# A graph layer on one core: 48 instead of 42 edge tiles gathered row by row, and another order of loads and writes on SyncE's queue

## The chip, the cores and the metric

The kernel runs on one core of a Trainium2 chip. The metric is the device time in microseconds of one execution; lower is better. The core's engines are named as the profile names them: PE (TensorE, with PEld its weight loads), DVE (VectorE), ACT (ScalarE), POOL (GpSimd) and SP (SyncE). PEq, ACTq, POOLq and SPq are the instruction queues of the engines; SP does no arithmetic here and only issues transfers.

## The reference

A message-passing layer over 6,250 nodes and 206,250 edges, sorted by receiver (`dst`), 128 channels in 8 heads of 16. Cut to what matters:

```python
w_ij  = silu(edge_feats @ rad_W1 + rad_b1) @ rad_W2 + rad_b2
w_ij += silu(chi_scalar @ sph_W1 + sph_b1) @ sph_W2 + sph_b2
q_i, k_j, v_j = (x @ Wq)[dst], (x @ Wk)[src], (x @ Wv)[src]
alpha = (q_i * w_ij * k_j).sum(per head) / sqrt(16) * edge_weight
out = segment_sum(alpha * v_j, dst) / 16
result = layernorm(x + out)
```

All arithmetic that matters is float32.

## The kernel before

**Tiles.** 128 edges are a tile, four tiles a quad (403 quads), four quads a group (101 groups). The main loop runs over groups `g` and, in each, over four slots, which take the quads in the order 0, 2, 1, 3 (`order`, line 138). Instructions go onto each engine's queue in the order in which the Python text emits them; each queue is worked off in order, so that an instruction that waits holds everything behind it on its queue.

**A quad.** `first_layers` (PE, `ph`) and `silus` (ACT) make the hidden edge features, `q_at_edges` (PE, `pq`) spreads the receivers' queries over the edges with the one-hot matrix `hotT`, `weigh` (PE, `pw`) makes the edge weights, `multiply`, `scores` and `messages` (DVE) make the messages out of `pq`, `pw` and `kv`, and a group later `sum_quads` (PE, `po`) adds them up by receiver. `sum_group`, `part_sums`, `moments`, `roots` and `normalize` finish a group's 128-row block of the result; four blocks are normalized together.

**Senders' rows.** K and V of all nodes lie as 1 KB rows in a DRAM table `kv_tab`, made in the prologue. For each tile POOL issues one indirect transfer (`gather`, line 132) that fetches 128 rows. `gathers` issues a quad's four tiles 14 quads ahead of their use (`AHEAD`), into a ring of 16 quads (`RING`). The first ten quads get K and V from gathered rows of `x` instead, in the prologue.

**Tiles loaded singly.** In `ROW_TILES` quads, spread evenly over the places 20 to 392 of the order (`row_at`, line 139), the fourth tile isn't gathered: `gathers` issues three transfers, and `load_rows` has the 128 rows fetched by 128 transfers of one row each (line 191, tile `wide`). SP issues 80 of them in batches of 32, 32 and 16, each behind a load of the addresses into registers (`at_i`, line 186); ACT issues 48 in two batches of 24, a few in each slot: two between its two SiLUs (`next_rows(2)`) and up to `ROW_SLOT_ACT - 2` at the end of the slot (`rows_at_end`). A tile's single rows are issued over the slots since the tile before it, ending eight slots ahead of its use (`ROW_LEAD`).

**The rest of SP's queue.** In each group SP also issues `load_x` (slot 0: a register load of the group's place from `gb_i`, line 280, then 64 KB of `x`), `load_feats` (slot 2, three groups ahead, 512 KB), `load_rel` (slot 2, two groups ahead, the receivers `relb`, 128 KB, from which DVE makes `hotT` in `one_hots_T`, line 264, in slot 1 of the group before the one that uses it), and `write_rows` (line 708: one finished block of 64 KB in every slot as long as there is one). Blocks are written at places that may overlap, so each write waits until the write before it has landed. `load_x` and `load_feats` also wait for a matrix product of the slot before (`past`).

Of the kernel before, what the change touches and what calls it, by code (L numbers as in the profile page):

```python
# [12 lines left out]
F32 = mybir.dt.float32  # L13
BF16 = mybir.dt.bfloat16
# [7 lines left out]
SP = mybir.EngineType.SP  # L22
# [3 lines left out]
P = 128  # L26
N = 6250
D = 128
# [7 lines left out]
NG = math.ceil(E / (P * GT))  # L36
NT = NG * GT
EG = P * GT
EQ = P * QT
# [6 lines left out]
ROW_BYTES = 2 * D * 4  # L46
XQ = 10
RING = 16
ROW_TILES = 42
ROW_FIRST = 20  # L50
ROW_LAST = 392
ROW_LEAD = 8
ROW_UNIT = 32
ROW_ACT = 48
ROW_UNIT_ACT = 24
ROW_SLOT_ACT = 6
ROW_SEMS = 8
CHECK = 20
XL = 3
NEIGHBORS = 16.0  # L60
EPS = 1e-5
SCALE = 1.0 / (math.sqrt(HD) * NEIGHBORS)


@with_exitstack
def gnn_kernel(ctx, tc, x, src, dst, weight, edges, rad_W1, rad_b1, rad_W2, rad_b2,
# [14 lines left out]
    nc = tc.nc  # L81
# [11 lines left out]
    src_x = const.tile([P, math.ceil(XQ / NQ) * GT], I32, name="src_x")  # L93
    at_i = const.tile([ROW_TILES, P], I32, name="at_i")
    scale = const.tile([P, NT], F32, name="scale")
# [14 lines left out]
    gb_i = const.tile([1, NG], I32, name="gb_i")  # L110
# [8 lines left out]
    gp = ctx.enter_context(tc.tile_pool(name="group", bufs=2))  # L119
# [18 lines left out]
    order = [g * NQ + j for g in range(NG) for j in (0, 2, 1, 3) if g * NQ + j < QUADS]  # L138
    row_at = [ROW_FIRST + (n + 1) * (ROW_LAST - ROW_FIRST) // ROW_TILES for n in range(ROW_TILES)]
    row_quads = {order[i] for i in row_at}  # L140
# [10 lines left out]
    def rows_at_end():  # L151
        n = ROW_SLOT_ACT - 2
        m = min(n, len(act_now))
# [6 lines left out]
    r_of = {}  # L160
    feats_of, relb_of, act_of, kv_of, hot_of, hotT_of, x_of, q_of, msg_of = ({} for _ in range(9))
# [11 lines left out]
    def load_rows(i):  # L173

        k = next((k for k in range(ROW_TILES) if i <= row_at[k] - ROW_LEAD), None)
        start = len(order) if k is None else (row_at[k - 1] if k else ROW_FIRST) - ROW_LEAD + 1
# [45 lines left out]
    def load_feats(g, mark=None):  # L222
        feats_of[g] = gp.tile([P, EG // 2], F32, name="feats", bufs=3)
        o = nc.sync.dma_start(feats_of[g], edges[g])
        if mark is not None:
            tc.add_manual_dep(o.ins, mark.ins.name, WAIT, reason="one signal of TensorE a quad")
# [3 lines left out]

    def load_rel(g):

        relb_of[g] = gp.tile([P, EQ], BF16, name="relb")
        r = rel_lin[g * GT:(g + 1) * GT, :].rearrange("(j t) e -> j (t e)", j=NQ)
        nc.sync.dma_start(relb_of[g], r[:, None, :].to_broadcast([NQ, W, EQ]))

# [40 lines left out]

    def load_x(g, mark=None):

        r_of[g] = nc.values_load(gb_i[:1, g:g + 1], engines=(SP,), min_val=0, max_val=(N - P) * D * 4,  # L280
                                 skip_runtime_bounds_check_because="the table is clamped to it")
        x_of[g] = gp.tile([P, D], F32, name="x", bufs=XL + 4)
        o = nc.sync.dma_start(x_of[g].bitcast(U8), rows_from(x, r_of[g]))
        if mark is not None:
            tc.add_manual_dep(o.ins, mark.ins.name, WAIT, reason="one signal of TensorE a quad")
# [21 lines left out]
    with tc.tile_pool(name="nodes", bufs=1) as nodes, \  # L307
# [76 lines left out]

        rows_f = nodes.tile([P, ROW_TILES], F32, name="rows_f")

# [6 lines left out]
        def turn_rows():  # L393
            pt = nps.tile([P, QT, P], F32, name="pt", bufs=3)
            nc.tensor.transpose(pt[:ROW_TILES, 0, :], rows_f, ident)
            nc.vector.tensor_copy(at_i, pt[:ROW_TILES, 0, :])

# [64 lines left out]
        n = len(chunks)  # L462
# [49 lines left out]
    with tc.tile_pool(name="ps", bufs=1, space=PSUM) as pp:  # L512
# [27 lines left out]
        def first_layers(q):  # L540

            return [hidden_of(q, i) for i in range(2)][-1]
# [162 lines left out]
        def write_rows(n=1):  # L705
            for _ in range(min(n, len(written))):
                g, y = written.pop(0)
                nc.sync.dma_start(rows_from(out, r_of.pop(g)), y.bitcast(U8))
# [24 lines left out]
        written = []  # L733
        load_feats(1)
        load_rel(1)
        load_feats(2)
        for g in range(1, XL):
            load_x(g)
# [7 lines left out]
        for g in range(NG - 1):  # L746
            for slot, j in enumerate((0, 2, 1, 3)):
                q = g * NQ + j
                i = g * NQ + slot
                turned, past, old = None, mark, marks  # L750
                if slot == 0 and g == CHECK + len(checks) + 1:
                    verdict()
                if slot == 0:
                    turned = turn_q(g + 1, pp.tile([P, EQ], F32, name="pq", bufs=2))
                if slot == 1 and 2 <= g:
                    turned = sum_group(g - 2)
                if slot == 2:
                    turned = make_q(g + 1, pp.tile([P, EQ], F32, name="pq", bufs=2))
                if 1 <= g:
                    for t in ((), (0, 1), (2,), (3,))[slot]:  # L760
                        mark = sum_quads(g - 1, t)
                first_layers(order[i + 2])
                mark = q_at_edges(order[i + 1])
                marks = weigh(order[i + 1])
                silus(order[i + 2], mark, marks, lambda: next_rows(2))
                if turned:
                    turned()
                if 1 <= g and slot == 3:
                    part_sums(g - 1)
                if i + AHEAD < len(order):  # L770
                    gathers(order[i + AHEAD], old[-QT:])
                multiply(order[i + 1], mark)
                messages(q, scores(q, marks=marks), marks=marks)
                if slot == 0:
                    if g + XL < NG:
                        load_x(g + XL, past)
                if slot == 2:
                    if g + 3 < NG:
                        load_feats(g + 3, past)
                    if g + 2 < NG:  # L780
                        load_rel(g + 2)
                if slot == 1:
                    one_hots_T(g + 1)
                    if g + 2 < NG:
                        pick(g + 2)
                    if 1 <= g:
                        place(g - 1)
                write_rows()
                if slot == (3 if g < NG - 2 else 2):
                    if 2 <= g:  # L790
                        statistics(g - 2)
                if slot == 3:
                    if g + 1 < NG - 1:
                        one_hots(g + 1)
                    if CHECK <= g < CHECK + len(checks):
                        checks[g - CHECK]()
                if g == NG - 3 and slot in (0, 2):
                    wide_one_hots(order[slot // 2 - 3])
                if g == NG - 2 and slot == 0:
                    wide_one_hots(order[-1])  # L800
                    n = nc.values_load(general, min_val=0, max_val=1)
                    place(g)
                    place(NG - 1)
                if g == NG - 3 and slot in (1, 3):
                    weigh_wide(order[slot // 2 - 3])
                if g == NG - 2 and slot == 1:
                    weigh_wide(order[-1])
                load_rows(i)
# [56 lines left out]
    def general_group(g):  # L865
        with tc.tile_pool(name="lg", bufs=1) as lg, tc.tile_pool(name="lb", bufs=1) as lb, \
# [12 lines left out]
            for j in range(NQ):  # L879
                kv = lb.tile([P, QT, 2 * D], F32, name="kv_l")  # L880
# [41 lines left out]
                for t in range(QT):  # L922


                    d = dstf_g[:, j * QT + t:j * QT + t + 1]
                    pd = pp.tile([P, P], F32, name="pd")
                    nc.tensor.transpose(pd, d.to_broadcast([P, P]), ident)
                    same = lb.tile([P, P], F32, name="same")
                    nc.vector.tensor_scalar(same, pd, d, None, op0=OP.is_equal)
                    earlier = lb.tile([P, P], F32, name="earlier")  # L930
                    nc.vector.tensor_tensor(earlier, same, before, op=OP.mult)
                    to = lb.tile([P, 4], F32, name="to")
                    nc.vector.tensor_reduce(to[:, 0:1], earlier, AX.X, OP.max)
                    nc.vector.tensor_tensor(to[:, 1:2], spare, d, op=OP.subtract)
                    nc.vector.tensor_tensor(to[:, 2:3], to[:, 1:2], to[:, 0:1], op=OP.mult)
                    to_i = lb.tile([P, 1], I32, name="to_i")
                    nc.vector.tensor_tensor(to_i, to[:, 2:3], d, op=OP.add)
                    ps = pp.tile([P, D], F32, name="ps_l")
                    nc.tensor.matmul(ps, same, msg[:, t, :], start=True, stop=True)
                    part = lb.tile([P, D], F32, name="part_l")  # L940
                    nc.scalar.activation(part, ps, AF.Copy)
                    scatter_add(to_i, part)
# [72 lines left out]
```

## Time and profile before

| | |
|---|---|
| median of 3 runs | 1985.53 us (1983.56 to 1986.35) |
| the profiled execution's own time | 1985.41 us |
| its span in the profile, first to last instruction | 1983.3 us |
| busy: PE / POOL / DVE / ACT | 1782.5 / 1488.6 / 1471.1 / 752.2 us |
| gathers of `kv` and of `x` rows on POOL | 1530 and 40 |
| single rows issued by SP and by ACT | 3360 and 2016 |
| register loads of SP for these rows / for `x` | 126 / 101 |
| granted TensorE clock | 0.916 |

Busy time counts instructions of the engine proper; the issuing of transfers by SP and ACT is not in it, and POOL's busy time holds its gathers without what lies between them. A line in the list of waits reads: engine and line that waited, what it waited for, microseconds in total, number of times, longest. A timeline line reads: start, microseconds, engine, line, operation, tiles and number, and in brackets the idle time before it with what ended it.

### The profile page before, as it was taken

The numbers are of one execution on the slowest core, as the hardware profiler recorded it, in microseconds if no ns is written. First come the engines' busy times: TensorE is split into PE (matmuls) and PEld (weight loads), VectorE is DVE, ScalarE is ACT, GpSimd is POOL, SyncE is SP. The second block draws the span as 40 slices with busy tenths as digits, with TensorE's granted clock in tenths as the row PEclk, the third lists the DMA queues.
The fourth block names the chain that finished last, engine by engine and source line by source line (L and its number), as shares of the span: only waits on it lengthen the run. The fifth ranks groups of instructions, "written<-read, shape, count | busy, mean of one in ns | idle before, by whom it ended". The sixth has DMA issues, their size and how long they took to land.

```text
span 1983.3 us, 55295 instructions
## 1 busy us (share of the span) xinstructions
PE 1782.5 (90%) x16014; PEld 1505.7 (76%) x16014; DVE 1471.1 (74%) x3123; ACT 752.2 (38%) x1437; POOL 1488.6 (75%) x1580
## 2 busy tenths in 40 slices
PE   9899999978997988998898888899989988898897
PEld 7788788767876877876787777777767777777786
DVE  6687777768876877776777777767767767777777
ACT  3244344333343343342343333333433433433334
POOL 7777777777777777777777777777777777777775
PEclk9899899978998998998999889989989999898988
DMA  8545545455455555454554555545545455445543
GB/s 316 160 141 156 157 145 156 142 157 156 143 157 154 146 156 154 144 160 139 159 158 140 159 142 155 158 143 154 154 145 158 144 152 159 142 142 158 157 140 90
DMA packets 150194, 304.77 MB, mean 154 GB/s; under 512 B 38732, under 2 KB 83900, under 8 KB 149884
## 3 DMA queue, kind: packets, MB, share of 16 engines
q0 software_dynamic: 74720, 203.26, 36.7%
q1 hardware_dynamic: 69632, 95.45, 14.8%
q10 hardware_dynamic: 5532, 2.47, 0.5%
q8 instruction: 128, 2.10, 0.4%
q14 instruction: 182, 1.49, 0.3%
HBM read 287.58 MB, written 13.46 MB: 152 GB/s over the span
## 4 chain that ended last, share of the span: by engine, by line
PE 56%; DMA 17%; DVE 11%; issue 6%; POOL 3%; ACTq 2%; SPq 2%; ACT 2%; DVEq 0%; POOLq 0%
PE pw L565 28%; DMA kv<-kv_tab,src_i 14%; PE pq L527 10%; PE ph L518 7%; PE po L616 4%; DVE kq L577 4%; DMA relb<-rel_lin 3%; PE pw L560 3%; ACTq L191 2%; POOL msg L132 2%; DVE side L587 2%; DVE kq L585 2%; SPq L191 1%; PE pq L657 1%; POOL kv L132 1%
## 5 line engine op out<-in xcount | busy, mean ns | idle before, releaser
L132 POOL DMA_INDIRECT kv<-kv_tab,src_i x1530 | 1447.9, 946 | 466.6 <-PE pw L565 174.2
L548 ACT ACTIVATE act<-ph,b 128x512 f32<-128x512 f32 x806 | 546.5, 687 | 1091.0 <-PE pq L527 1003.5
L565 PEld LDWEIGHTS pw<-w,act 128*128 128x128 f32 x6448 | 822.8, 207 | 105.6 <-issue 94.7
L565 PE MATMUL pw<-w,act 128*128 128x128 f32 x6448 | 902.7, 298 | 0.0
L527 PE MATMUL pq<-q,hotT 32*128 32x128 f32 x3224 | 502.9, 299 | 50.8 <-DVE hotT L264 40.4
L518 PE MATMUL ph<-feats,w 32*128 32x512 f32 x1612 | 501.2, 680 | 31.5 <-ACT act L548 30.6
L527 PEld LDWEIGHTS pq<-q,hotT 32*128 32x128 f32 x3224 | 422.8, 200 | 75.9 <-issue 55.4
L577 DVE TENSOR_TENSOR kq<-pq,kv 128x512 f32<-128x512 f32 (+1 forms) x403 | 271.8, 674 | 243.8 <-PE pq L527 121.2
L587 DVE TENSOR_REDUCE side<-kq 128x32 f32<-128x512 f32 x403 | 280.1, 695 | 43.2 <-DVE kq L585 1.4
L604 DVE TENSOR_TENSOR msg<-kv,side 128x512 f32<-128x512 f32 (+1 forms) x404 | 271.9, 673 | 42.7 <-DVE side L591 1.2
L585 DVE TENSOR_TENSOR kq<-pw,kq 128x512 f32<-128x512 f32 x403 | 274.7, 682 | 0.0
L518 PEld LDWEIGHTS ph<-feats,w 32*128 32x128 f32 x1612 | 137.9, 193 | 113.7 <-issue 58.2
L560 PE MATMUL pw<-brow,onesb 3*128 3x512 bf16 x403 | 161.9, 402 | 9.4 <-DVE kq L585 9.3
L616 PE MATMUL po<-msg,hot 128*32 128x128 f32 x3200 | 154.6, 290 | 0.0
L264 DVE TENSOR_TENSOR hotT<-relb,side 128x512 f32<-128x512 bf16 x101 | 69.0, 683 | 97.5 <-DMA relb<-rel_lin 97.4
L657 PE MATMUL pq<-part,to 128*128 128x128 f32 x200 | 45.9, 313 | 82.6 <-DVE kq L577 58.0
L591 DVE TENSOR_TENSOR side<-side,scale 128x32 f32<-128x32 f32 x400 | 80.0, 200 | 42.3 <-DVE side L587 0.5
L657 PEld LDWEIGHTS pq<-part,to 128*128 128x128 f32 x200 | 31.3, 197 | 93.0 <-issue 54.0
L616 PEld LDWEIGHTS po<-msg,hot 128*32 128x32 f32 x3200 | 71.3, 111 | 38.3 <-issue 4.8
L269 DVE TENSOR_TENSOR hot<-rel,side 128x512 f32<-128x512 f32 x100 | 66.1, 661 | 0.0
L258 PE MATMUL pq<-wq,xT 128*128 128x128 f32 x200 | 42.9, 299 | 11.2 <-DVE kq L577 11.1
L132 POOL DMA_INDIRECT msg<-in_x,src_x x40 | 38.9, 972 | 13.3 <-issue 11.6
(117 smaller groups left out, 855.6 us busy)
## 6 DMA issues: line engine op xcount, KB each, us to landing
wide<-kv_tab SPq DMA_DIRECT2D x3360, 1.0 KB
feats<-in_edges SPq DMA_DIRECT2D x101, 512.0 KB
wide<-kv_tab ACTq DMA_DIRECT2D x2016, 1.0 KB
kv<-kv_tab,src_i POOLq DMA_INDIRECT x1530
relb<-rel_lin SPq DMA_DIRECT2D x101, 128.0 KB
x<-in_x SPq DMA_DIRECT2D x101, 64.0 KB
out<-y SPq DMA_DIRECT2D x101, 64.0 KB
kv_tab<-kv SPq DMA_DIRECT2D x12, 512.0 KB
```

What stands on the lines that cost most here:

```text
L132: return nc.gpsimd.indirect_dma_start(out=o, out_offset=None, in_=table, in_offset=bass.IndirectOffsetOnAxis(ap=index, axis=0))
L518: return nc.tensor.matmul(act_of[q, i], w1[r0:r0 + R, :], feats_of[g][r0:r0 + R, c0:c0 + EQ], start=True, stop=True)
L527: o = nc.tensor.matmul(pq_of[q][:, t, :], hotT_of[g][b, t * P:(t + 1) * P], q_of[g][b, :], start=True, stop=True)
L548: o = nc.scalar.activation(act, act_of[q, i], AF.Silu, bias=b1[:, i:i + 1])
L560: nc.tensor.matmul(pw, onesb, brow.rearrange("p t d -> p (t d)"), start=True, stop=False)
L565: o = nc.tensor.matmul(pw[:, t, :], act_of[q, i][:, t * P:(t + 1) * P], w2[:, i, :], start=False, stop=(t == QT - 1 and i == 1))
L577: o = nc.vector.tensor_tensor(kq_of[q][:, u, :], pq_of[q][:, u, :], kv[:, :, :D], op=OP.mult)
L585: nc.vector.tensor_tensor(m, pw_of[q][:, t, :], m, op=OP.mult)
L587: o = nc.vector.tensor_reduce(alpha, m.rearrange("p t (h e) -> p t h e", e=HD), AX.X, OP.add)
L604: o = nc.vector.tensor_tensor(msg_of[q][:, u, :].rearrange("p t (h e) -> p t h e", e=HD), kv[:, :, D:].rearrange("p t (h e) -> p t h e", e ...
L616: o = nc.tensor.matmul(po_of[g][j * W:(j + 1) * W, :], hot_of[g][:, j * QT + t, :], msg_of[g * NQ + j][:, t, :], start=(t == 0), stop=(t = ...
L657: nc.tensor.matmul(ph[:, :D], to[:n, 0, :], part[:n, :], start=True, stop=(g == 0))
```

## The change

Six things change together. (1) `ROW_TILES` goes from 42 to 48: six more tiles are fetched row by row, by SP and ACT, and six fewer gathers are issued by POOL; the single tiles lie 7.75 places apart instead of 8.86. (2) `ROW_SLOT_ACT` goes from 6 to 7: ACT issues up to five rows at the end of a slot instead of four. (3) `load_rel` runs three groups ahead instead of two, with three buffers of `relb` instead of two. (4) `load_feats` moves from slot 2 to slot 3. (5) `write_rows` is called in slot 1 only, one block per group, apart from the last groups. (6) `load_x` loads the places of four groups (`XB`) with one register load, and no longer waits for `past`. A scratch tile of the path for unsorted input, which isn't taken with these inputs, shares memory with another.

```diff
-ROW_TILES = 42
+ROW_TILES = 48
-ROW_SLOT_ACT = 6
+ROW_SLOT_ACT = 7
+XB = 4
...
     def load_rel(g):
-        relb_of[g] = gp.tile([P, EQ], BF16, name="relb")
+        relb_of[g] = gp.tile([P, EQ], BF16, name="relb", bufs=3)
...
     def load_x(g, mark=None):
-        r_of[g] = nc.values_load(gb_i[:1, g:g + 1], engines=(SP,), min_val=0, max_val=(N - P) * D * 4,
-                                 skip_runtime_bounds_check_because="the table is clamped to it")
+        if g not in r_of:
+            n = min(XB, NG - g) if g else 1
+            _, at = nc.values_load_multi_w_load_instructions(
+                gb_i[:1, g:g + n], engines=(SP,), min_val=0, max_val=(N - P) * D * 4,
+                skip_runtime_bounds_check_because="the table is clamped to it")
+            r_of.update(zip(range(g, g + n), at))
...
         load_rel(1)
+        load_rel(2)
         load_feats(2)
...
-                if slot == 0:
-                    if g + XL < NG:
-                        load_x(g + XL, past)
-                if slot == 2:
-                    if g + 3 < NG:
-                        load_feats(g + 3, past)
-                    if g + 2 < NG:
-                        load_rel(g + 2)
+                if slot == 0 and g + XL < NG:
+                    load_x(g + XL)
+                if slot == 2 and g + 3 < NG:
+                    load_rel(g + 3)
+                if slot == 3 and g + 3 < NG:
+                    load_feats(g + 3, past)
...
-                write_rows()
+                if slot == 1 or g >= NG - 2:
+                    write_rows()
...
-                    same = lb.tile([P, P], F32, name="same")
+                    same = kv[:, 0, :D]
```

## The prediction

> **What bounds the kernel now.** I began with the shares of the engines and the slices of the page, went from there to POOL's groups and its timeline, then to the waits and the chain, and last to SP's queue. The page shows PE as the busiest engine and POOL at 75%:
>
> ```profile
> span 1983.3 us, 55295 instructions
> PE 1782.5 (90%) x16014; PEld 1505.7 (76%) x16014; DVE 1471.1 (74%) x3123; ACT 752.2 (38%) x1437; POOL 1488.6 (75%) x1580
> POOL 7777777777777777777777777777777777777775
> L132 POOL DMA_INDIRECT kv<-kv_tab,src_i x1530 | 1447.9, 946 | 466.6 <-PE pw L565 174.2 <-issue 172.3 <-DMA kv<-kv_tab,src_i 46.0
> L132 POOL DMA_INDIRECT msg<-in_x,src_x x40 | 38.9, 972 | 13.3 <-issue 11.6 <-DMA src_x<-in_src 1.4 <-DMA msg<-in_x,src_x 0.3
> ```
>
> The shares mislead; the slices do not. POOL has a 7 in every slice but the last, while PE's share moves. POOL's timeline, at its start and its end:
>
> ```profile
> 3.04 1.10 POOL L132 DMA_INDIRECT msg<-in_x,src_x  x1 [1.43 <-DMA src_x<-in_src]
> 57.94 0.95 POOL L132 DMA_INDIRECT kv<-kv_tab,src_i  x1 [0.30 <-issue]
> ...
> 1966.14 0.94 POOL L132 DMA_INDIRECT kv<-kv_tab,src_i  x1 [0.30 <-PE pw L565]
> 1967.39 0.94 POOL L132 DMA_INDIRECT kv<-kv_tab,src_i  x1 [0.30 <-issue]
> 1968.74 0.47 POOL L674 TENSOR_TENSOR y<-tot,x 128x128 f32<-128x128 f32 x1 [0.42 <-ACT tot L661]
> ```
>
> Neighbours start 1.25 us apart: 0.95 of gather and 0.30 between, whatever name stands in the bracket. From 3.04 to 1967.39 lie 1569 steps (1530 + 40 - 1), or 1.252 us each over the whole run, prologue included. So the 466.6 us of idle time is 0.30 after every gather, a fixed part of its price and no wait. POOL issues gathers back to back from start to end, and the end follows 15.9 us behind the last gather (1983.3 - 1967.4). The time is the number of gathers times 1.25 us, plus 19 us of start and tail.
>
> The waits look as if something else were worth more:
>
> ```profile
> DVE hotT L264 <- DMA relb<-rel_lin: 97.4, 26, 12.3
> ACT act L548 <- PE pq L527: 1003.5, 359, 13.2
> ...
> DVE hotT L264 <- DMA relb<-rel_lin: 59.1, 13, 10.3
> ...
> DVE kq L577 <- DMA kv<-kv_tab,src_i: 45.2, 28, 3.7
> ...
> PE pw L565 28%; DMA kv<-kv_tab,src_i 14%; PE pq L527 10%; PE ph L518 7%; PE po L616 4%; DVE kq L577 4%; DMA relb<-rel_lin 3%; PE pw L560 3%; ACTq L191 2%; POOL msg L132 2%; DVE side L587 2%; DVE kq L585 2%; SPq L191 1%; PE pq L657 1%; POOL kv L132 1%
> ...
> L560 PE MATMUL pw<-brow,onesb x11: 376/376/603, 66.5 to 109.1; 3*128 3x512 bf16 x11
> ...
> 109.73 1.98 PE pw L565 x16
> 113.56 1.98 PE pw L565 x16
> ```
>
> The first two lines are of the whole run, the third of the stretch 500 to 1000 us, the fourth of 1500 to 1984; then come the chain by line, the first eleven edge products on PE (up to 110 us), and two pieces of the chain. DVE loses 97.4 us to late receivers, and the chain counts 3% for them, some 60 us. But while it stalled in the first half, POOL did not. The rows that PE, DVE and ACT work on had been gathered long before: quad 10 was complete in POOL's queue at 57.94, and PE reached its eleventh edge product only at 109.1, so compute starts some 50 us behind POOL, with a ring of 16 quads to be behind in. It gains on POOL until it waits for gathers themselves (the fourth line). The stalls delay only that catching up.
>
> Undisturbed, compute takes 3.8 us a quad (109.73 to 113.56); POOL takes 5.0 for four gathers. Compute has room, unless SP feeds it too slowly. That is the question of this change.
>
> **SP's queue.** Its waits and issues between 200 and 900 us, a stretch of its timeline, and its register loads:
>
> ```profile
> SPq L708 <- DMA out<-y: 53.5, 20, 4.8
> SPq L224 <- PE pw L565: 5.8, 15, 0.7
> ...
> wide<-kv_tab SPq DMA_DIRECT2D x1339, 1.0 KB
> relb<-rel_lin SPq DMA_DIRECT2D x37, 128.0 KB
> ...
> 427.01 10.76 SPq L191 DMA_DIRECT2D wide<-kv_tab  x32
> 437.87 0.37 SPq L224 DMA_DIRECT2D feats<-in_edges  x1
> 438.33 0.58 SPq L235 DMA_DIRECT2D relb<-rel_lin  x1
> 439.08 5.60 SPq L708 DMA_DIRECT2D out<-y  x2
> 445.40 0.35 SPq L283 DMA_DIRECT2D x<-in_x  x1
> 446.91 5.22 SPq L191 DMA_DIRECT2D wide<-kv_tab  x16
> ...
> L186 SPq TENSOR_LOAD <-at_i x126: 979/1924/2497, 122.9 to 1877.2; - x126
> L280 SPq TENSOR_LOAD <-gb_i x101: 271/544/883, 24.1 to 1892.9; - x101
> ```
>
> A single tile costs SP 2 x 10.76 + 5.22 = 26.7 us of rows and three address loads, 3 x 1.92 = 5.8, together 32.5 us. A group also costs 0.37 + 0.58 + 0.35 + 0.40 for features, receivers, x and one written block (the written block's 0.40 from the 5.60 for two with a wait between them is an estimate), with some 0.1 for the small instructions at each: 2.1 us. To that come 0.54 for the place of x and 53.5 / 37 = 1.45 of waiting for the block written before.
>
> - Before, tiles 8.86 quads apart: SP 32.5 x 4 / 8.86 = 14.7, + 2.1 + 0.54 + 1.45 = **18.8 us a group**; the trace agrees, 37 groups in 700 us are 18.9. POOL: (16 - 4 / 8.86) x 1.25 = **19.44**.
>
> So SP is nearly as full as POOL, and the late receivers are SP running behind: it is the next bound, 3% away.
>
> **The change, part by part.**
>
> (1) Six fewer gathers: 6 x 1.25 = **-7.5 us** on POOL, all of it on the path, since POOL never waits. On SP each group now costs 32.5 x 4 / 7.75 = 16.8 us for rows, +2.1. On DVE a split tile costs more, from these rows:
>
> ```profile
> L577 DVE TENSOR_TENSOR kq<-pq,kv 128x512 f32<-128x512 f32 x361 | 248.5, 688 | 218.7 <-PE pq L527 102.4 <-DMA kv<-kv_tab,src_i 80.1 <-PE pw L565 26.3
> L577 DVE TENSOR_TENSOR kq<-pq,kv 128x384 f32<-128x384 f32 x42 | 23.3, 555 | 25.1 <-PE pq L527 18.8 <-DMA kv<-kv_tab,src_i 5.7 <-PE pw L565 0.3
> L577 DVE TENSOR_TENSOR kq<-pq,wide 128x128 f32<-128x128 f32 x42 | 11.8, 282 | 0.0
> 1036.24 0.55 ACTq L191 DMA_DIRECT2D wide<-kv_tab  x2
> ```
>
> 555 + 282 - 688 is 0.15 us, twice (scores' input and messages), six times: 1.8 us, hidden in the 45 us that DVE waits for gathers late in the run. Where compute lagged, it would cost at most those 1.8.
>
> (2) ACT issues 6 x 48 rows more, at 0.28 us (0.55 for two): 81 us, 0.2 a slot. It lies inside the 1003.5 us in which ACT waits for `pq`, 2.5 us a slot. Behind those rows on ACT's queue stand the next SiLUs, and PE waits for them; the slots with a normalization have the least room there, and compute's 1.2 us a quad over POOL covers them. I count nothing.
>
> (3) Receivers a group sooner: four slots, about 19 us, more than the longest stall of 12.3. The buffer it now waits for was read by DVE a group and more before; no one is queued behind a new wait. The stalls of DVE go; worth nothing to the end by itself. Late next are the features, now a slot later: seven slots, some 34 us, ahead of their use, which SP may lag.
>
> (4) Features move past one slot's rows on SP and their mark is a slot later; 0.37 us of issue, unchanged. When SP is ahead it waits there for PE, with rows queued behind; when it is behind, the mark is long past (5.8 us in 700 now).
>
> (5) One block a group: each follows the last by some 19 us, and the longest wait was 4.8, so 1.45 a group goes. In its place the fourth block of a batch leaves six slots before DVE needs its buffer, some 29 us; an SP that lags more than about 24 stalls DVE there, once in four groups.
>
> (6) Places: one load of four registers in four groups. Not in the trace; between 0.54 (one register) and 0.98 (16, the shortest of the address loads), nearer to the first. I take 0.7, so 0.2 a group for 0.54.
>
> SP after: 16.8 + 2.1 + 0.2 = **19.1 us a group**, POOL (16 - 4 / 7.75) x 1.25 = **19.35**. The relief, 1.45 + 0.34, all but pays for 2.1 more of rows; 0.25 a group is in hand.
>
> The sum against the profiled execution: 1985.4 - 7.5 = 1977.9. It lies 0.1 under the median of the runs shown, so **1978.0**.
>
> **Rivals.** *SP becomes the bound, and it is slower.* The margin is 1.3%, and the batches scatter by more. SP carries rows through some 93 groups (from quad 13 to 384). It may lag compute by about 25 us (the 29 to 34 above less some 5 of landing), and compute can make up about 20 at the end, where 18 quads have no rows to be issued (18 x 1.2): together 45 of the 50 it starts behind. So it decides at SP = POOL: above about 19.35 us a group each 0.1 costs 9.3 us. At 19.6 (row or load 3% dearer) it would be 1978 + 0.25 x 93 = 2001. Against it: the same sum met the measured 18.9, and none of its prices hangs on the number of tiles. For it: no other queue is so full. The Trainium skill, "DMA: Bandwidth & Descriptors", section "Rules for kernel authors", says to coalesce many small transfers into one, under 64 KB being mostly overhead: here a 128 KB gather becomes 128 rows of 1 KB, which is this rival's direction. The trace agrees that size hardly counts in the issue: 0.34 us for a row, 0.35 for 64 KB of x. Chance 0.11.
>
> *SP just misses.* At 19.39 to 19.47 the gain is given back in part, or wholly: 1981.5 to 1989. Chance 0.07.
>
> *Nothing gained, transfers bind.* If the transfers themselves set the pace, moving their issue to other queues changes nothing: 1985.4. The same page, section "Issuing engines are not separate DMA queues", says this: it only saves the sequencer's time, usually small beside the transfer. The trace speaks against it: the sixteen DMA engines are busy about half of the time in all slices but the first.
>
> ```profile
> DMA  8545545455455555454554555545545455445543
> ```
>
> By that rule a change of time needs a full sequencer, and POOL's is one. Chance 0.02.
>
> *The receivers are the bound.* Taking the chain's 3% at its word, 60 us and the 7.5 would go: 1918. POOL's unbroken steps contradict it. Chance 0.01. That the gathers don't drop out is no case: `gathers` issues three for every quad in `row_quads`.
>
> **The numbers.** The forecast has 0.79. Its own range is 1976 to 1980 (the mean step of 1.252 or 1.25, tail unchanged within 2 us). The range must leave out at most 2 in 10: 1975.5 to 1986 holds the forecast, the transfer rival and half of the near miss, and leaves the slow case out. A difference under 0.2% (4 us) can't be told from none here: faster than 1981.5 has 0.79 + 0.01 = 0.80, within 0.2% has 0.08, slower than 1989.5 has 0.12.
>
> **What the profile after would show.** Right: 1524 gathers of `kv`, still 1.25 us apart, the last starting near 1960, a tail near 16 us; DVE's wait for `relb` a few us instead of 97.4; SP's wait for `out` near nothing; 3840 rows on SP; more DVE waiting for `kv`, and earlier in the run. Wrong: gathers more than 1.3 us apart for long, or a tail over 20 us; DVE or PE waiting for `feats`, `wide` or a written block up to the end, with SP never idle and over 19.35 us from one `feats` to the next.

## The result and the profile after

| | before | after |
|---|---|---|
| median, six runs each | 1985.49 us (1983.56 to 1986.83) | 1999.07 us (1995.64 to 2002.71) |
| ratio, 95% interval | | 1.0069 (1.0056 to 1.0082) |
| span of the profiled execution | 1983.3 us | 1993.9 us |
| last gather starts | 1967.39 us | 1959.64 us |
| span behind the last gather | 15.9 us | 34.2 us |

The changed kernel is slower by 13.6 us, where 1978.0 was forecast. The profiled execution of after, at 1995.64 us, is the fastest of its six; its span is 10.6 us longer. The page of after, in the lines that answer to those shown of before:

```profile
span 1993.9 us, 56782 instructions
PE 1760.0 (88%) x16014; PEld 1499.3 (75%) x16014; DVE 1468.4 (74%) x3141; ACT 752.0 (38%) x1437; POOL 1482.8 (74%) x1574
POOL 7777777777777777777777777777777777777772
...
PE pw L570 27%; PE pq L532 10%; PE ph L523 8%; SPq L192 7%; DMA feats<-in_edges 7%; PE po L621 4%; DMA kv<-kv_tab,src_i 3%; PE pw L565 2%; DVE kq L582 2%; DVE side L592 2%; SPq L187 2%; ACTq L192 2%; DMA x<-in_x 2%; POOL msg L133 2%; DVE kq L590 2%
L133 POOL DMA_INDIRECT kv<-kv_tab,src_i x1524 | 1442.0, 946 | 464.7 <-PE pw L570 175.9
```

POOL has its 7 in every slice but the last, which holds a 2 where before had a 5. In the chain, SP's rows (`SPq L192`) went from 1% to 7%, `feats` is new with 7%, `kv` fell from 14% to 3%. POOL's timeline at the end:

```profile
1958.38 0.95 POOL L133 DMA_INDIRECT kv<-kv_tab,src_i  x1 [0.30 <-issue]
1959.64 0.94 POOL L133 DMA_INDIRECT kv<-kv_tab,src_i  x1 [0.30 <-issue]
1978.62 0.46 POOL L679 TENSOR_TENSOR y<-tot,x 128x128 f32<-128x128 f32 x1 [18.04 <-ACT tot L666]
```

The gathers still start 1.25 us apart and the last starts 7.75 us earlier: the six gathers that are gone brought their price. Then POOL waits 18.04 us for ACT's `tot` of the last block; before, that wait was 0.42. The kernel ends with compute, and compute is late. The waits of the whole run say for what:

```profile
PE ph L523 <- DMA feats<-in_edges: 118.1, 34, 11.6
...
PE pq L250 <- DMA x<-in_x: 36.2, 12, 5.8
...
DVE kq L582 <- DMA kv<-kv_tab,src_i: 20.9, 14, 6.3
...
DVE hotT L265 <- DMA relb<-rel_lin: 16.2, 6, 4.2
```

The receivers cost 16.2 us instead of 97.4. PE now waits for features, 34 times, and for `x`: the transfers that SP issues. DVE's wait for gathers fell from 85.8 (80.1 + 5.7, its two `kq` rows in the prediction) to 20.9: compute hardly ever comes up to POOL. The granted clock is lower too, 0.908 against 0.916, but PE was busy for 1760.0 us against 1782.5, which speaks against a slower PE as what makes compute late. SP's timeline in the middle, from the features of one group to those of the next (28.1 us, since two batches of 32 rows fall into this group):

```profile
420.64 0.43 SPq L225 DMA_DIRECT2D feats<-in_edges  x1
423.34 10.76 SPq L192 DMA_DIRECT2D wide<-kv_tab  x32
434.28 0.36 SPq L288 DMA_DIRECT2D x<-in_x  x1
434.81 0.38 SPq L713 DMA_DIRECT2D out<-y  x1
437.55 10.40 SPq L192 DMA_DIRECT2D wide<-kv_tab  x32
448.05 0.56 SPq L236 DMA_DIRECT2D relb<-rel_lin  x1
448.70 0.44 SPq L225 DMA_DIRECT2D feats<-in_edges  x1
```

Between the issues lie register loads (some 2.3 us ahead of each 32 rows) and little else. SP's costliest entry of waits from 200 to 900 us, then, of the whole run, its single rows and its loads:

```profile
SPq L225 <- PE pw L570: 6.2, 19, 0.5
...
wide<-kv_tab SPq DMA_DIRECT2D x3840, 1.0 KB
...
L187 SPq TENSOR_LOAD <-at_i x144: 973/2091/2537, 122.9 to 1915.2; - x144
...
L283 SPq TENSOR_LOAD <-gb_i x26: 503/1074/1158, 24.2 to 1884.6; - x26
```

SP hardly waits. Added up from the trace from the features of group 14 to those of group 94, its time for one group, against what the prediction had put down:

| us a group | predicted | measured |
|---|---|---|
| rows and their loads | 16.8 | 13.78 + 2.99 = 16.77 |
| features, receivers, x, one block, small instructions | 2.1 | 0.46 + 0.62 + 0.49 + 0.52 + 0.19 = 2.28 |
| places of x | 0.2 | 0.30 |
| sum | 19.1 | 19.35 |
| POOL's pace | 19.35 | 19.38 (15.48 gathers x 1.252) |

(The same sum over before gives 18.97, of it 1.1 of waiting, predicted as 18.8.) The whole margin of 0.25 was in small terms, and SP needs for a group just the time that POOL needs.

What that does is seen in the lag, that is, how far compute lies behind POOL: the start of a quad's first product `kq` less the start of that quad's last gather, worked out from the two timelines. For the last quad, from DVE's timeline of before and then of after, these are the two products (the gathers, 1967.39 and 1959.64, are shown above):

```profile
1971.38 0.69 DVE L577 TENSOR_TENSOR kq<-pq,kv 128x512 f32<-128x512 f32 x1
```

```profile
1981.26 0.69 DVE L582 TENSOR_TENSOR kq<-pq,kv 128x512 f32<-128x512 f32 x1
```

| lag at quad, us | 10 | 42 | 90 | 138 | 210 | 386 | 402 |
|---|---|---|---|---|---|---|---|
| before | 51.9 | 35.5 | 30.4 | 12.5 | 6.0 | 3.2 | 4.0 |
| after | 51.9 | 24.0 | 24.2 | 21.3 | 25.6 | 21.6 | 21.6 |

Both start 52 us behind. Before reaches POOL near quad 178 and follows it. After gains faster at first, has 28 us made up by quad 42, and then hardly more: from there SP sets compute's pace, at POOL's own speed. The lag it keeps, 21.6 - 4.0 = 17.6 us, less 7.75 of gathers, is 9.9 of the 10.6 us of span; the rest is in the last blocks.

### The profile page after: what moved, and what is told of

Read it like the earlier page. It is cut to its first block, busy times and chain, and to the rows that moved or that the text cites. A ratio compares the mean times of both kernels' runs of the same rounds, so it can differ in the third digit from the quotient of the medians.

```text
span 1993.9 us, 56782 instructions
## 1 busy us (share of the span) xinstructions
PE 1760.0 (88%) x16014; PEld 1499.3 (75%) x16014; DVE 1468.4 (74%) x3141; ACT 752.0 (38%) x1437; POOL 1482.8 (74%) x1574
## 4 chain that ended last, share of the span: by engine, by line
PE 55%; DMA 12%; SPq 10%; DVE 10%; issue 7%; ACTq 2%; POOL 2%; ACT 2%; DVEq 0%; POOLq 0%
PE pw L570 27%; PE pq L532 10%; PE ph L523 8%; SPq L192 7%; DMA feats<-in_edges 7%; PE po L621 4%; DMA kv<-kv_tab,src_i 3%; PE pw L565 2%; DVE kq L582 2%; DVE side L592 2%; SPq L187 2%; ACTq L192 2%; DMA x<-in_x 2%; POOL msg L133 2%; DVE kq L590 2%
## 5 line engine op out<-in xcount | busy, mean ns | idle before, releaser
L553 ACT ACTIVATE act<-ph,b 128x512 f32<-128x512 f32 x806 | 546.4, 687 | 1127.2 <-PE pq L532 992.3
L523 PE MATMUL ph<-feats,w 32*128 32x512 f32 x1612 | 509.4, 689 | 154.4 <-DMA feats<-in_edges 118.1
L265 DVE TENSOR_TENSOR hotT<-relb,side 128x512 f32<-128x512 bf16 x101 | 68.8, 681 | 16.4 <-DMA relb<-rel_lin 16.2
L250 PE MATMUL pq<-pick,x 128*128 128x128 f32 x200 | 41.7, 291 | 36.2 <-DMA x<-in_x 36.2
L250 PEld LDWEIGHTS pq<-pick,x 128*128 128x128 f32 x200 | 31.2, 197 | 38.7 <-DMA x<-in_x 36.1
```

The lines of the kernel that those rows point to most:

```text
L523: return nc.tensor.matmul(act_of[q, i], w1[r0:r0 + R, :], feats_of[g][r0:r0 + R, c0:c0 + EQ], start=True, stop=True)
L553: o = nc.scalar.activation(act, act_of[q, i], AF.Silu, bias=b1[:, i:i + 1])
```

## The experiments

The theories, by the letters used in some expectations: **S**, SP's queue has become the bound; **F**, it is the features' place in the queue, a slot later, that makes them late; **A**, ACT's rows hold up the SiLUs; **E**, one of the edits other than the tiles costs the time by itself. The runs were made on three chips (e1 to e4, e5 to e8, e13 and e14), on which the kernel before took 1985.51, 1989.51 and 1985.04 us; all ratios are to it on the same chip, with a 95% interval. "SP" is its time a group, added up as above, with the waits that it holds where they are over 0.2. The last gather scatters by some 5 us between profiles of kernels with 48 tiles (e2 apart), so only the ratios are read to the microsecond. e2 and e4 have one batch of 16 rows more in the 80 groups counted than the change, which is 0.07 us a group of their "SP".

| kernel | SP, us a group | lag at quad 386, us | last gather, us | ratio |
|---|---|---|---|---|
| before | 18.97, waits 1.1 | 3.2 | 1967.39 | 1 |
| e1, 42 tiles | 19.10, waits 1.7 | 5.3 | 1969.29 | 1.0003 (0.9994 to 1.0013) |
| after, the change | 19.35 | 21.6 | 1959.64 | 1.0069 (1.0056 to 1.0082) |
| e2, tiles alone | 20.85, waits 1.0 | 63.8 | 2052.79 | 1.0679 (1.0657 to 1.0700) |
| e3, receivers from ACT | 18.83, waits 0.3 | 4.8 | 1963.56 | 0.9965 (0.9952 to 0.9977) |
| e4, features in slot 2 | 19.63 | 35.5 | 1963.28 | 1.0151 (1.0128 to 1.0173) |
| e5, 46 tiles | 18.94, waits 0.4 | 5.3 | 1965.33 | 0.9976 (0.9967 to 0.9986) |
| e6, 56 rows on ACT | 18.91, waits 1.1 | 3.7 | 1962.75 | 0.9966 (0.9956 to 0.9977) |
| e7, places singly | 19.51 | 31.1 | 1964.86 | 1.0116 (1.0099 to 1.0133) |
| e8, 52 tiles | 18.98, waits 0.4 | 6.5 | 1959.53 | 0.9949 (0.9933 to 0.9966) |

### e1: the change with 42 tiles

```diff
-ROW_TILES = 48
+ROW_TILES = 42
```

> All of the change but the six tiles: 42 tiles, the other five parts as they are after. Theory S (SP's queue sets the pace of the changed kernel): SP costs 32.8 x 4 / 8.86 = 14.8 for rows, + 2.3 + 0.3 = 17.4 us a group against POOL's 19.44, so POOL is the bound as before: 1985.5, within 2 us; DVE's 97 us of waits for relb gone, its waits for kv starting before 500 us. Rival E (the edits beside the tiles cost the time: the features a slot later, the block written once a group, ACT's fifth row): slower than 1985.5 by most of the 21 us between 1999 and the 1978 of POOL's sum, so 2000 to 2006.

Measured: 1986.24 us against 1985.51. At 42 tiles all the other edits together cost nothing and bring nothing, so E falls. From its waits:

```profile
DVE kq L582 <- DMA kv<-kv_tab,src_i: 164.6, 100, 4.1
```

Compute now waits for gathers 100 times, and its lag is 5.9 us at quad 90 already (30.4 before): the freed SP time makes compute catch up a hundred quads earlier, and the end does not move, as POOL sets it.

### e2: the tiles alone, the rest as before

```diff
 (in the kernel before)
-ROW_TILES = 42
+ROW_TILES = 48
-ROW_SLOT_ACT = 6
+ROW_SLOT_ACT = 7
```

> The kernel before with 48 tiles and ACT's fifth row, nothing else of the change. Theory S: SP costs 16.9 + 2.3 + 0.64 + 1.45 = 21.2 us a group, 1.9 over POOL, and over 93 groups 175 us are lost, part of it already in the kernel after: 2150 to 2190, with SP never idle and DVE waiting for relb. Rival E: the tiles alone bring their 7.5 us, or lose little: 1978 to 1990.

Measured: 2121.05 us, 135.5 over before. Its waits, and a piece of POOL's timeline:

```profile
DVE hotT L264 <- DMA relb<-rel_lin: 365.3, 60, 17.8
...
1001.50 0.95 POOL L132 DMA_INDIRECT kv<-kv_tab,src_i  x1 [0.30 <-issue]
1004.05 0.94 POOL L132 DMA_INDIRECT kv<-kv_tab,src_i  x1 [1.60 <-PE pw L565]
```

The direction is S's, the size some 30 us under its lowest value: SP took 20.85 us a group and not the 21.2 by which the expectation was worked out. Here compute falls so far behind (64 us) that the ring of gathered quads is full and POOL has to wait, 1.60 us before the second gather: the last gather starts 85 us later than before's. So the other edits are needed; without them the six tiles cost ten times what they cost in the change.

### e3: the receivers issued by ACT

```diff
-        nc.sync.dma_start(relb_of[g], ...)
+        (nc.scalar if g > 2 else nc.sync).dma_start(relb_of[g], ...)
```

> After, with the receivers of groups 3 and up issued on ACT's queue instead of SP's: 0.67 us a group less on SP, the same transfers. Theory S: SP 19.4 - 0.7 = 18.7 us a group against POOL's 19.35, compute makes up its 25 us behind the gathers in 40 groups: 1978, within 2 us. Rival E: nothing of its causes is touched: 1999, within 3. Rival A (ACT's rows hold up PE): 0.6 us more on ACT a group, the same or slower, 1999 to 2005.

Measured: 1978.46 us against 1985.51, the time forecast for the change itself. From its waits:

```profile
DVE kq L582 <- DMA kv<-kv_tab,src_i: 125.8, 85, 3.8
...
PE ph L523 <- DMA feats<-in_edges: 15.0, 9, 5.5
```

Taking 0.62 us a group from SP, 3% of its work, brings the whole gain back: features are late for 15.0 us instead of 118.1, compute is at POOL's heels from quad 114 on. The transfers are the same, so it is their issue that was late, not the time that they take. ACT got more work and the kernel became faster, which speaks against A.

### e4: the features back in slot 2

```diff
                 if slot == 2 and g + 3 < NG:
+                    load_feats(g + 3, past)
                     load_rel(g + 3)
-                if slot == 3 and g + 3 < NG:
-                    load_feats(g + 3, past)
```

> After, with the features back in slot 2, ahead of the receivers. Theory S: SP costs what it costs, 19.4 us a group; the features may come one slot later against their use, but rows, x and receivers are as late, so SP may lag 2 to 5 us more: 1994 to 1998. Rival F (the features a slot later are the whole loss, the 118 us of PE's waits for them): 1978 to 1982.

Measured: 2014.44 us, slower than the change by 0.8%. Neither theory had this: F expected a gain and falls, S expected the time to stay. Its waits:

```profile
DVE hotT L265 <- DMA relb<-rel_lin: 110.7, 33, 8.5
...
PE pq L250 <- DMA x<-in_x: 88.7, 30, 7.0
PE ph L523 <- DMA feats<-in_edges: 73.8, 24, 7.4
```

Issued earlier, the features are late for less time, the receivers behind them and `x` for more. But the order has a price of its own: SP took 19.63 us a group, 0.28 more than with the same instructions in the change's order. Of this, 0.07 is the batch more that is counted, and 0.14 lies in the address loads (3.13 instead of 2.99). Why the loads are dearer is taken up at the end.

### e5 and e6: less work for SP in two ways

```diff
 (e5)
-ROW_TILES = 48
+ROW_TILES = 46
 (e6)
-ROW_ACT = 48
+ROW_ACT = 56
-ROW_SLOT_ACT = 7
+ROW_SLOT_ACT = 8
```

> After with 46 tiles (8.09 quads apart), the rest as after. Theory S: rows and their loads, 16.8 a group at 48 tiles, fall to 16.8 x 7.75 / 8.09 = 16.1, with 2.6 of the rest 18.7 us a group against POOL's 19.38; four gathers fewer than before show in full: 1980.5, within 2. If the loss grew with the number of tiles by itself (each tile costing 21 / 6 = 3.5 us beyond its gather), 46 tiles would give 1978 + 2.5 + 14 = 1994.

> After with eight of SP's 80 rows in each tile given to ACT (56 instead of 48, up to eight a slot): SP issues 72 rows in 32, 32 and 8. Theory S: (72 x 0.334 + 2 x 2.1 + 0.8) x 4 / 7.75 = 15.0, + 2.6 = 17.6 us a group: 1978, within 2. Rival A (ACT's rows hold up PE and so the end): one more row in each slot, 1999 or slower.

Measured: e5 1984.75 and e6 1981.84 us, both against 1989.51 on that chip, so -4.8 and -7.7. The expectations were worked out from 1985.5 for before; taken as differences, -5.0 and -7.5, both are met. Four gathers fewer at 1.25 are 5.0 us, six are 7.5: with SP's work below POOL's pace the time is POOL's sum again. e6 puts still more rows on ACT, so A falls.

### e7: the places of x singly

```diff
-XB = 4
+XB = 1
```

> After with one register load of a place for each group again (XB = 1), the rest as after: 0.65 instead of 0.30 us a group, so SP 19.7. Theory S: SP is above POOL by 0.35 a group for some 90 groups: 30 us more than after, 2025 to 2035. If SP had room, or the loss came from elsewhere: 1999, within 3.

Measured: 2011.45 us against 1989.51, +22. The direction is S's, the size isn't: by the ratios this is 9 us more than the change, and 30 were expected. The single loads cost 0.58 us a group instead of 0.30, but the address loads became cheaper by 0.12 (2.88 instead of 2.99), so SP stood at 19.51 and not at the 19.7 of the expectation. Its wait for features is the change's, a little longer:

```profile
PE ph L523 <- DMA feats<-in_edges: 126.7, 37, 10.7
```

### e8: more tiles, with e3 and e6

```diff
-ROW_TILES = 48
+ROW_TILES = 52
-ROW_ACT = 48
+ROW_ACT = 56
-ROW_SLOT_ACT = 7
+ROW_SLOT_ACT = 9
-        nc.sync.dma_start(relb_of[g], ...)
+        (nc.scalar if g > 2 else nc.sync).dma_start(relb_of[g], ...)
```

> After with the receivers on ACT's queue (from group 3), 56 rows of a tile on ACT, up to nine a slot, and 52 tiles (7.15 quads apart). Theory S: SP (72 x 0.334 + 2 x 2.1 + 0.8) x 4 / 7.15 = 16.3, + 1.9 = 18.2 us a group against POOL's 19.30; ten gathers fewer than before: 1973, within 3. Rival A: nine issues and the receivers leave ACT too little room, PE waits for SiLUs more and compute falls behind POOL: 1985 or slower.

Measured: 1978.35 us against 1989.51, -11.2: faster than both kernels. From its waits:

```profile
ACT act L553 <- PE pq L532: 615.8, 229, 8.9
...
DVE kq L582 <- DMA kv<-kv_tab,src_i: 114.6, 66, 5.4
```

POOL is the bound (compute waits for gathers), and ten gathers at 1.25 would be 12.5 us, 1.3 more than came, within the 3 that the expectation allowed. ACT, on which the work was put, still waits 615.8 us for `pq`, of 992.3 in the change.

### e13 and e14: the last two tiles left out, and the change again

The first 46 tiles lie where the change has them; the last tile is at place 376 instead of 392. e14 is the change itself on the same chip. (The same pair was run twice before, as e9 and e10 on one chip and e11 and e12 on another. There every kernel, before too, took a third longer, and SP 26.0 to 26.5 us a group. e13's kernel was 1.0321 and 1.0289 of before there, the change 1.0290 and 1.0328. The four expectations, which were those given here, were all missed, and these runs don't tell the two kernels apart.)

```diff
 (e13)
-ROW_TILES = 48
+ROW_TILES = 46
-    row_at = [ROW_FIRST + (n + 1) * (ROW_LAST - ROW_FIRST) // ROW_TILES for n in range(ROW_TILES)]
+    row_at = [ROW_FIRST + (n + 1) * (ROW_LAST - ROW_FIRST) // 48 for n in range(ROW_TILES)]
```

> After with the first 46 of its 48 tiles at their places, the last single tile at quad 376 instead of 392. SP 19.35 us a group as after, its rows ending 16 quads sooner; POOL's sum 5 us under before. If compute catches up once SP is done (3.9 us a quad against 5.0): 1 to 3 us under before. If it can't gain at the end: 13 to 16 us over before, as after has it.

> The changed kernel as it is, on the same chip as the run before it: 10 to 14 us over before.

Measured: e13 1986.39 us, ratio 1.0011 (1.0002 to 1.0021); e14 1997.84 us, ratio 1.0068 (1.0051 to 1.0084); before 1985.04. The expectation for e13 was missed by 2 to 4 us: it is 1.3 us over before. In its profile this isn't the catching up, since its span behind the last gather is before's, 16.0 us against 15.9. It is POOL's pace: over the whole run its gathers start 1.2549 us apart, before's 1.2520, which over 1565 steps is 4.5 us. Why they are dearer stays open. But SP's time a group is the change's (19.36 us), and compute still lags by 19.8 us at quad 376 (in the change by 26.1 there and by 21.6 ten quads on). From DVE's timeline, products eight quads apart, and from POOL's, its end:

```profile
1891.93 0.69 DVE L582 TENSOR_TENSOR kq<-pq,kv 128x512 f32<-128x512 f32 x1
...
1922.40 0.68 DVE L582 TENSOR_TENSOR kq<-pq,kv 128x512 f32<-128x512 f32 x1
...
1966.82 0.94 POOL L133 DMA_INDIRECT kv<-kv_tab,src_i  x1 [0.30 <-PE pw L570]
1967.85 0.47 POOL L679 TENSOR_TENSOR y<-tot,x 128x128 f32<-128x128 f32 x1
```

With SP's rows at an end, compute does a quad in 30.47 / 8 = 3.81 us; the lag falls from 19.8 at quad 376 over 15.4 at 384 to 5.7 at 392 and 3.7 at the end, and POOL goes on to `y` without a wait. So the late end of the change is the lag that SP's rows keep up: 16 places without rows remove 16 us of it.

## Why the prediction was wrong

The bound of the kernel before, POOL with SP next and 3% away, was read rightly, and so was most of the working. The signs that the prediction gave for its being wrong are those that came: a tail over 20 us (34.2), PE waiting for features, and SP hardly idle at 19.35 us a group. By its points:

- *Six gathers less, -7.5:* right, the last gather starts 7.75 earlier.
- *Rows on SP, 16.8:* right, 16.77. The split tiles on DVE and the rows on ACT at nothing: right as far as shown, since e6 and e8 have more of ACT's rows and gain.
- *Receivers' stalls go, the features are late next:* right, 97.4 to 16.2 us, and 118.1 for features. *One block a group ends the waiting on SP:* right, 53.5 us in 700 before, no entry over 6.2 after.
- *Small issues at 2.1 and places at 0.2:* **the step that failed first.** They were 2.28 and 0.30. The load of four registers was taken at 0.7, nearer to one register (0.544) than to the shortest load of sixteen (0.979); the median is 1.074, above both ends of the bound. Of the 2.1, the four issues were 1.70 and measure 1.76; the small instructions and gaps around them were put down as 0.1 at each, 0.4 together, and come to 0.52. With rows 0.03 cheaper the whole is 0.25 more, which is all that was in hand.
- *Compute makes up about 20 us in the last 18 quads:* **the step that failed next**, and it turned a tie into a loss. The prediction's slow rival let SP go as slowly as POOL at no cost: of the 50 us that compute starts behind, SP could lag by 25 and compute make up 20 at the end. The first part held: 52 - 24 = 28 us were gone by quad 42. The second brought 24.2 - 21.6 = 2.6 us or less. From SP's timeline at the end, and DVE's share from there on by windows:

```profile
1916.87 5.17 SPq L192 DMA_DIRECT2D wide<-kv_tab  x16
1922.14 0.36 SPq L225 DMA_DIRECT2D feats<-in_edges  x1
...
1925.00:1955.00 30.00, 28.84 (x279) 24.32 (x278) 27.14 (x61) 13.51 (x28) 22.69 (x25) 1.00 0.54 166
```

The columns of the last row are the stretch, its length and the busy time of PE, PEld, DVE, ACT and POOL, then the granted clock, the DMA share and GB/s. The quads without rows are counted by places in compute's order, but SP itself issued late: its last rows left it at 1922, when compute had come to quad 389. In what remained DVE was busy 27.14 of 30 us, at 4.4 us a quad (1932.4 at quad 392 to 1950.0 at 396); 2.5 of these are the one-hot tiles of the last groups (`wide_one_hots`), which fall there. The last six quads took 5.2 us each, slower than POOL's 5.0; what holds them was not followed. The other late kernels gain as little: from quad 392 to 402 the lag falls by 1.6 us in e2 and by 2.5 in e4. The room was between SP's last rows and quad 392; e13 had it, the change did not.

So the rival "SP becomes the bound" is what happened, but at 19.35, the point where it was to begin to decide, and not at 19.6. To end at POOL's sum, compute has to make up all 20 us while rows are still being issued, over some 93 groups: SP must stay 20 / 93 = 0.2 below POOL's 19.38, under about 19.2. That is an estimate from the lag table; no run whose SP hardly waits lies between 18.98 and 19.35 to test it. Above the tie the price of 9.3 us for each 0.1 was somewhat high. From the change to e2 (1.43 more without the batch that is counted beyond the change's, 121 us by the ratios) it is 8.5, to e4 (0.21 more in the same way, 16 us) 7.6, and to e7 (0.16 more, 9 us by the ratios, 12 by the medians) 6 to 8.

The Trainium skill, "DMA: Bandwidth & Descriptors", section "Issuing engines are not separate DMA queues", which the prediction weighed, says that issuing from several engines saves only the sequencer's time for it, usually small beside the DMA itself. The trace agrees: the receivers take 0.62 us of SP's time and landed 4.0 to 5.3 us after their issue in the six cases in which DVE waited for them. But where the sequencer is the bound, small isn't little: with 0.62 us a group off SP, e3 went from 1.0069 to 0.9965 of before, some 20 us.

## What to carry to other kernels

A queue that only issues transfers shows no busy time, so add up its instructions for one round of the loop, small ones and register loads too, and compare the sum with the pace of the bound; where the margin is smaller than the sum of the terms that were guessed (here 0.25 of 19.35), call it a tie. At a tie the late start was not made up here: ask where, in time and not in places of the order, the follower can gain on the leader. Here SP's issues could be moved to ACT, the engine that waits longest, and each gather less was then worth POOL's price again (e3, e6, nearly so in e8).

## What was not expected of the hardware

The price of a register load differs with what its queue issued just before. The means of the 32-register address loads on SP, sorted from the traces between 200 and 1850 us by the transfer issued ahead of them:

| us, load of 32 registers behind | x | features | block | receivers |
|---|---|---|---|---|
| before | 1.91 | | 2.09 | 2.42 |
| after | 2.08 | 2.12 | 2.16 | 2.43 |

The 16-register loads of after go from 1.13 behind x to 1.56 behind the receivers. The receivers are the one transfer that reads the same bytes for many partitions. So a load costs up to 0.5 us more behind one transfer than behind another, where the whole margin was 0.25 us a group. e4's trace bears that out: the loads that stood behind the features now stand behind the receivers, 44 of the 88 loads of 32 registers instead of 23, at 2.44 us each, while the other means are the change's within 0.06. With those of 16 registers that is 0.12 of the 0.14 us a group by which its loads are dearer. e7's loads were cheaper for another reason: the transfers ahead are the change's, but behind x and the block, in the groups that also load a place, a load takes 1.92 and 2.00 us. The change shows the same: behind x 1.96 in groups that load places (four loads) and 2.11 in the others (18). That a load is cheaper soon after another one is read from these means; no run tests it by itself. The Trainium skill, "DMA: Bandwidth & Descriptors", section "Latency and other measured facts", gives a floor of some 600 ns for such a load; here the single loads of before go down to 271 ns, below that floor, and 32 registers take four times as much as it behind the receivers.
